# Two layers of graph convolution by dense count matrices: early gathers moved within the first tile, and the third sum's opening reordered

## The chip, the cores and the metric

The kernel runs on one core of one Trainium2 chip. The metric is device time in microseconds (us) of one execution. The core has five engines that run side by side: PE (TensorE, matrix products; PEld is its weight load), DVE (VectorE), ACT (ScalarE), POOL (GpSimd, which here issues the indirect gathers) and SP (SyncE, which here issues most other transfers). Each engine works through its own instructions in a fixed order, and an instruction whose data are not there holds up everything behind it on its engine.

## The reference

The graph has 6,250 nodes with 64 features and 206,250 directed edges (100,000 drawn ones, both ways, and one loop for each node), sorted by destination. Cut to what matters:

```python
h = relu(layernorm(x))
a = segment_sum(h[src], dst)                    # first sum
h = relu(relu((h + a) @ W1 + b1) @ W2 + b2)
a = segment_sum(h[src], dst)                    # second sum
x = x + relu((h + a) @ W3 + b3) @ W4 + b4
h = relu(layernorm(x))
y = relu(relu(h @ WM1 + bM1) @ WM2 + bM2) @ WM3 + bM3
z = segment_sum(y[src], dst)                    # third sum
out = x + relu(relu(concat(h, z) @ WU1 + bU1) @ WU2 + bU2) @ WU3 + bU3
```

The three sums run over the same edges. The message network of the second convolution depends on the source node alone, so it is computed per node.

## The kernel before

A sum over edges is a product with a matrix of counts, `A`, whose cell says how often an edge joins two nodes. The nodes make 49 tiles of 128. The kernel builds `A` tile by tile in bytes, uses each tile at once for the first sum, and stores it to DRAM (L429); the second and third sums read it back.

**Building.** A half tile of 64 destinations has its edges in a window of at most 120 neighbouring edges, and so 25 gather steps of 128 windows serve the 49 tiles. They come in thirteen batches (one step, then two each). For a batch `search` (L291) finds by ACT, among samples of `dst`, the block of 550 edges in which a window starts (L298), and DVE writes `row` and `base` (L302, L303). `fetch_blocks` (L306) lets POOL gather the blocks `blk` (L311). `search_block` (L315) counts in the block by ACT (L322). `fetch_edges` (L326) lets DVE compute the offset (`off_f` L331, `off` L332) and POOL gather the edges themselves (`d_win`, `s_win`, L336). `slots` (L342) takes them apart on DVE (from `pair`, L359), `cast` and `turn` bring them into `lkw`. For each tile `hot` makes one-hot patterns on DVE (`there` L400, `high` L404, `low` L407), PE counts by 64 products (`cnt`, L423), ACT evicts the counts (`a`, L425), and PE multiplies the 49 pieces of the tile with `hp`, the normalised features in three bfloat16 parts (`acc`, L566). `values` (L487) makes `hp` from `x` for seven tiles at a time: a norm, and `split` (L244 to L248), alternating between ACT and DVE.

**What sets the order.** Python code emits the instructions in a certain order; `beside` holds, for each quarter of each tile, the steps of later batches that are emitted beside it. A scheduler of the tile framework then fixes the order on each engine by data and by its own estimate of durations; `follow`, `behind` and `placed` tie some instructions to others. POOL's queue takes the gathers in the resulting order.

Batches in the start: the searches and gathers of batches 0 to 2 are emitted ahead of the first tile, with the values of five of the seven strips of `x`. Beside tile 0 come the last two strips, `search_block` and `fetch_edges` of batch 2, `search` and `fetch_blocks` of batch 3, and `search` of batch 4. Beside tile 1 (batch 1 in `beside`) come `search_block` and `fetch_edges` of batch 3 and `fetch_blocks` of batch 4.

**Second and third sum.** `sweep` goes over groups of four tiles (eleven of them, then one of three and one of two, L77). A group has 13 pieces of four steps each, the last with one step (the last group has six of eight steps and one of one). For a piece SP loads the counts as bytes (`a`, L731; five buffers), ACT or DVE widens them (`ar`, L735; six buffers), and PE multiplies (L742). A group sums in one PSUM bank, of two in `pacc`. After a group come its layers: `conv2` after the second sum, in six parts, and `conv3` after the third, in four; a part is emitted after so many further pieces as the tuple `after` says. `conv2` leaves `yr`, the stationary operand of the third sum; `conv3` frees its bank by ACT's copy (L697) and DVE's addition into `hz` (L698), and ends in an output transfer (L710). In the third sum the last two pieces of groups 0 and 1 wait until both groups' other eleven are done, because they need `yr` of the last five tiles. The layers of the last group of each sum are emitted after the sweep, all parts one after the other. The pool `f_pmix`, two banks that the first part uses, lies idle in the sweeps.

Of the kernel before, what the change touches and what calls it, by code (L numbers as in the profile page):

```python
# [151 lines left out]
def fast(ctx: ExitStack, tc: tile.TileContext, x, src, dst, w, bad, out):  # L152
# [138 lines left out]
    def search(b, after=None):  # L291

        if b >= len(BATCHES):
            return
        each, qs = tiles_of(b)
        for q in each:
            junk = wins.tile([P, NB], BF, name="junk", bufs=1)
            op = nc.scalar.activation(junk, smp, AF.Sign, bias=below_node[:, q:q + 1], accum_out=sign1[:, q:q + 1])  # L298
            if after:
                behind(op, after)  # L300
            follow(op, "ACT")
        nc.vector.tensor_scalar(row[:, qs], sign1[:, qs], -0.5, NB / 2 - 1, op0=OP.mult, op1=OP.add)  # L302
        return op, nc.vector.tensor_scalar(base[:, qs], sign1[:, qs], -0.5 * BLK, (NB / 2 - 1) * BLK + BLK / 2,  # L303
                                           op0=OP.mult, op1=OP.add)
# [10 lines left out]
    def search_block(b, i):  # L315

        if b >= len(BATCHES):
            return
        q = starts[b] + i
        blk = blks.pop(q)  # L320
        junk2 = wins.tile([P, BLK], BF, name="junk2", bufs=1)
        op = nc.scalar.activation(junk2, blk, AF.Sign, bias=below_node[:, q:q + 1], accum_out=sign2[:, q:q + 1])  # L322
        follow(op, "ACT")
        return op

    def fetch_edges(b):  # L326

        if b >= len(BATCHES):
            return
        each, qs = tiles_of(b)  # L330
        nc.vector.scalar_tensor_tensor(off_f[:, qs], sign2[:, qs], -0.5, base[:, qs], op0=OP.mult, op1=OP.add)  # L331
        nc.vector.tensor_scalar(off[:, qs], off_f[:, qs], float(E - P), None, op0=OP.min)  # L332
        lists[b] = [wins.tile([P, MOST, P], I32, name=name)[:, :len(each), :] for name in ("d_win", "s_win")]
        for win, of in zip(lists[b], (dst, src)):
            for i, q in enumerate(each):
                nc.gpsimd.indirect_dma_start(  # L336
                    out=win[:, i, :], out_offset=None, in_=of.rearrange("(a o) -> a o", o=1),
                    in_offset=bass.IndirectOffsetOnAxis(ap=off[:, q:q + 1], axis=0))
# [148 lines left out]
    def values(t):  # L487
        h = work.tile([P, XT, D], FP, name="h")
        begun, centered, squared = norm(h, t, XT)
        if t <= XT:  # L490
            behind(begun, sampled)
            behind(begun, bounds)
            behind(squared, searched[0])
        if t == XT:
            behind(centered, searched[1])
        split(hp[:, t:t + XT], h, XT, D)
# [3 lines left out]
    for b in range(len(BATCHES)):  # L500
        step = BATCHES[b]

        def at(u, what, *args):
            beside.setdefault(8 * starts[b] + u * step // 2, []).append((what, args))

        at(0, slots, b + 1)
        at(4, cast, b + 1, 0)
        at(5, cast, b + 1, 2)
        for i in range(BATCHES[b + 1] if b + 1 < len(BATCHES) else 0):
            at(7 + 2 * i, turn, b + 1, i)  # L510
        if b == 1:
            for i in range(BATCHES[3]):
                at(1 + i, search_block, 3, i)
            at(3, fetch_edges, 3)
            at(3, fetch_blocks, 4)
        if b > 0:
            at(6, search, b + 4)
            for i in range(BATCHES[b + 3] if b + 3 < len(BATCHES) else 0):
                at(10 + 2 * i, search_block, b + 3, i)
            at(13, fetch_edges, b + 3)  # L520
            at(14, fetch_blocks, b + 4)
# [24 lines left out]
    values(2 * XT)  # L546
    search(2, op)
    fetch_blocks(2)
    for t in range(3 * XT, 5 * XT, XT):
        values(t)  # L550

    r1, acc1 = {}, {}

# [32 lines left out]
    for t in range(NT + 1):  # L586
        last_total, total = total, FirstSum(t - 1, a) if t else None
        if t < NT:
            def between(i):
                if total:  # L590
                    total.quarter(i)
                if last_total and i == 2:
                    last_total.check()
                for what, args in beside.get(4 * t + i, ()):
                    what(*args)

            a = build(t, between)
            if t == 0:
                values(5 * XT)
                for i in range(2):  # L600
                    search_block(2, i)
                fetch_edges(2)
                values(6 * XT)
                search(3)
                fetch_blocks(3)
                search(4)
            if t == 1:
                w1p = weight_halves(w.w1x, "w1p", once)
                m1p = weight_halves(w.m1x, "m1p")
        else:  # L610
            last_total.check()
            for i in range(4):
                total.quarter(i)
            total.check()
# [8 lines left out]
    work = ctx.enter_context(tc.tile_pool(name="f_work2", bufs=2))  # L623
    narrow = ctx.enter_context(tc.tile_pool(name="f_narrow", bufs=5))
    wide = ctx.enter_context(tc.tile_pool(name="f_wide", bufs=6))
    pmix = ctx.enter_context(tc.tile_pool(name="f_pmix2", bufs=4, space=bass.MemoryType.PSUM))
    yr = late.tile([P, NT, 2, D], FR, name="yr")
    hz = late.tile([P, ROWS], FP, name="hz")

# [80 lines left out]
                queue.dma_start(out[ds(t0 * P, (k - 1) * P + m)].rearrange("(t p) d -> p t d", p=m),  # L710
                                o[:m, t0 - t:t0 - t + k, :])

    def sweep(stationary, self_too, late, single, then, after):

        accs = {}

        def width(g):

            return KC * (2 if GROUPS[g][1] <= 2 else 1)

        def piece(g, c):

            (t, n), k0 = GROUPS[g], c * width(g)
            if c == 0:
                accs[g] = pacc.tile([P, CH], FP, name="acc")
            acc = accs[g]
            m = min(width(g), H - k0)
            a = narrow.tile([P, 4 * KC * P], U8, name="a")[:, :n * m * P].rearrange("p (t b) -> p t b", t=n)  # L730
            nc.sync.dma_start(a, A[t:t + n, :, k0 * P:(k0 + m) * P].rearrange("t p b -> p t b"))  # L731
            ar = wide.tile([P, KC * 4 * P], FR, name="ar")[:, :m * n * P].rearrange("p (k t b) -> p k t b", t=n, b=P)
            widen = nc.scalar.copy if c % 5 in (1, 3) else nc.vector.tensor_copy
            order = "p k t b" if m % 2 == 0 else "p t k b"
            widen(ar.rearrange(f"p k t b -> {order}"), a.rearrange(f"p t (k b) -> {order}", b=P))  # L735
            for k in range(k0, k0 + m):
                if self_too and t <= k < t + n:
                    own = ar[:, k - k0, k - t, :]
                    nc.vector.tensor_tensor(own, own, w.ident, op=OP.add)
                parts = stationary(k)  # L740
                for i, part in enumerate(parts):
                    op = nc.tensor.matmul(acc[:, :n * P], part, ar[:, k - k0].rearrange("p t b -> p (t b)"),  # L742
                                          start=(k == 0 and i == 0), stop=(k == H - 1 and i == len(parts) - 1))
            swept[:] = [op]

        pieces, end = (H + KC - 1) // KC, len(GROUPS) - 1
        order = [(g, c) for g in range(end + 1) for c in range((H + width(g) - 1) // width(g))]
        if late:
            order[:2 * pieces] = sorted(order[:2 * pieces], key=lambda x: (x[1] >= pieces - 2, x))
        going = []  # L750
        for g, c in order:
            piece(g, c)
            for work_of in going:
                while work_of[1] and work_of[1][0] <= 0:
                    work_of[1].pop(0)
                    next(work_of[0], None)
                work_of[1] = [u - 1 for u in work_of[1]]
            if c == pieces - 1 and g < end - 1:
                going.append([then(*GROUPS[g], accs[g]), list(after)])
            elif g == end and c == 1:  # L760
                swept.clear()
                for _ in then(*GROUPS[end - 1], accs[end - 1]):
                    pass
        swept.clear()
        t, n = GROUPS[end]
        m = 1 if single else n
        works = [then(t + j, m, accs[end][:, j * P:(j + m) * P]) for j in range(0, n, m)]
        while works:
            works = [parts for parts in works if next(parts, works) is None]

    sweep(lambda k: [h2r[:, k, i, :] for i in range(2)], True, False, False, conv2, (0, 2, 5, 7, 9, 11))
    sweep(lambda k: [yr[:, k].rearrange("p i d -> p (i d)")], False, True, True, conv3, (0, 4, 8, 11))


@with_exitstack
# [248 lines left out]
```

## Time and profile before

| what | value |
|---|---|
| median of 3 runs | 888.64 us (888.33 to 889.93) |
| the profiled execution's own time | 890.53 us |
| its span, first to last instruction | 888.7 us |
| PE busy | 836.7 us (94%) |
| DVE busy | 636.3 us (72%) |
| ACT busy | 568.9 us (64%) |
| POOL busy | 119.2 us (13%) |
| products of second and third sum (L742) on the chain that ended last | 47% of the span |
| products of the first sum (L566) on it | 20% |

Busy time is an average over stages. The slices in the prediction cut the span into 40 parts of 22.2 us; a digit is the busy share in tenths, 9 meaning 90% or more. In a line of the timeline stand the start in us, the duration in us, engine, line, operation, what is written and read, how many instructions are merged, and in brackets the idle time before it with what ended it. "PEclk" and the granted clock are shares of TensorE's full clock. The first sum runs until about 382 us, the second until about 698, the third to about 880.

### The profile page before, as it was taken

The numbers are of one execution on the slowest core, as the hardware profiler recorded it, in microseconds if no ns is written. First come the engines' busy times: TensorE is split into PE (matmuls) and PEld (weight loads), VectorE is DVE, ScalarE is ACT, GpSimd is POOL, SyncE is SP. The second block draws the span as 40 slices with busy tenths as digits, with TensorE's granted clock in tenths as the row PEclk, the third lists the DMA queues.
The fourth block names the chain that finished last, engine by engine and source line by source line (L and its number), as shares of the span: only waits on it lengthen the run. The fifth ranks groups of instructions, "written<-read, shape, count | busy, mean of one in ns | idle before, by whom it ended". The sixth has DMA issues, their size and how long they took to land.

```text
span 888.7 us, 19590 instructions
## 1 busy us (share of the span) xinstructions
PE 836.7 (94%) x8202; PEld 727.9 (82%) x8202; DVE 636.3 (72%) x946; ACT 568.9 (64%) x768; POOL 119.2 (13%) x86
## 2 busy tenths in 40 slices
PE   0379999999999999999999999999999989999997
PEld 0369999999999999978888888888889867777786
DVE  6989999999999998635554545554556766677673
ACT  5557777767776666655555555555555677878873
POOL 3356544244322200000000000000000000000000
PEclk9989999999999999999999999999999999999998
DMA  6234343354443332745444444444435678898982
GB/s 146 74 137 160 148 172 135 135 184 149 158 147 139 123 146 111 220 107 134 122 122 127 124 123 122 130 111 127 130 96 135 168 195 208 237 244 235 248 219 67
DMA packets 192087, 133.57 MB, mean 150 GB/s; under 512 B 34965, under 2 KB 183317, under 8 KB 191989
## 3 DMA queue, kind: packets, MB, share of 16 engines
q1 hardware_dynamic: 185544, 121.19, 46.2%
q0 software_dynamic: 3600, 10.32, 4.1%
q8 instruction: 66, 1.08, 0.5%
q10 hardware_dynamic: 2844, 0.72, 0.4%
q14 instruction: 33, 0.26, 0.1%
HBM read 91.25 MB, written 40.94 MB: 149 GB/s over the span
## 4 chain that ended last, share of the span: by engine, by line
PE 88%; DVE 5%; DMA 3%; ACT 1%; issue 1%; POOL 1%; SPq 0%; ACTq 0%; POOLq 0%; DVEq 0%
PE acc L742 47%; PE acc L566 20%; PE cnt L423 8%; PE ps_t L445 6%; PE ps_y L454 4%; DVE low L407 1%; PE ps_g L484 1%; DMA blk<-in_dst_dram,row 1%; DVE high L404 1%; DVE there L400 1%; POOL s_win L336 1%; DMA d_win<-in_dst_dram,off 1%; ACT ar L735 1%; DMA xs<-in_x_dram 1%; PE tf L436 1%
## 5 line engine op out<-in xcount | busy, mean ns | idle before, releaser
L735 DVE CAST ar<-a 128x2048 fp32r<-128x2048 uint8 (+1 forms) x200 | 220.4, 1110 | 184.4 <-PE acc L742 157.0
L735 ACT CAST ar<-a 128x2048 fp32r<-128x2048 uint8 (+2 forms) x126 | 232.3, 1846 | 118.7 <-PE acc L742 100.0
L742 PE MATMUL acc<-ar,h2r 128*128 128x512 f32 (+2 forms) x1274 | 297.5, 388 | 0.0
L742 PEld LDWEIGHTS acc<-ar,h2r 128*128 128x128 f32 x1274 | 229.3, 188 | 49.7 <-issue 5.8
L566 PE MATMUL acc<-hp,a 128*128 128x193 bf16 x2401 | 239.1, 249 | 4.6 <-ACT a L425 2.3
L425 ACT ACTIVATE a<-cnt 128x784 int16<-128x784 f32 x196 | 161.0, 823 | 81.4 <-PE cnt L423 80.7
L566 PEld LDWEIGHTS <-a 128*128 128x128 fp8e4 x2401 | 198.9, 98 | 6.6 <-ACT a L425 2.9
L742 PE MATMUL acc<-ar,yr 128*128 128x512 f32 (+2 forms) x637 | 159.9, 402 | 2.5 <-DVE hz L698 1.3
L742 PEld LDWEIGHTS acc<-ar,yr 128*128 128x128 f32 x637 | 116.3, 190 | 35.2 <-issue 10.3
L423 PE MATMUL cnt<-high,low 128*128 128x49 bf16 x3136 | 113.8, 186 | 15.8 <-DVE low L407 13.2
L423 PEld LDWEIGHTS <-low 128*128 128x128 fp8e4 x3136 | 106.8, 96 | 23.5 <-DVE low L407 14.1
L407 DVE TENSOR_TENSOR low<-there,lkw 128x2048 int32<-128x2048 bf16 (+2 forms) x51 | 112.1, 2197 | 0.0
L404 DVE TENSOR_TENSOR high<-high,lkw 128x3136 bf16<-128x3136 bf16 (+2 forms) x51 | 87.7, 1720 | 15.0 <-PE cnt L423 14.5
L311 POOL DMA_INDIRECT blk<-in_dst_dram,row x25 | 53.4, 2137 | 90.6 <-DVE base L303 78.0
L400 DVE TENSOR_TENSOR there<-word,lkw 128x2048 bf16<-128x2048 bf16 (+2 forms) x51 | 59.0, 1173 | 0.0
L336 POOL DMA_INDIRECT d_win<-in_dst_dram,off x25 | 27.2, 1087 | 82.2 <-DVE pair L359 48.5
L336 POOL DMA_INDIRECT s_win<-in_src_dram,off x25 | 36.3, 1454 | 7.6 <-issue 7.6
L447 ACT ACTIVATE t<-ps_t,d 128x512 f32<-128x512 f32 (+2 forms) x26 | 17.3, 665 | 11.2 <-PE ps_t L445 11.1
L389 PE MATMUL ps_win<-identb,parts 128*128 128x128 bf16 x75 | 8.9, 225 | 15.7 <-ACT parts L381 15.7
L447 ACT ACTIVATE t<-ps_t,e 128x512 f32<-128x512 f32 (+2 forms) x28 | 17.6, 632 | 8.7 <-PE ps_t L445 8.7
L447 ACT ACTIVATE t<-ps_t,c 128x512 f32<-128x512 f32 (+1 forms) x26 | 17.1, 663 | 7.8 <-PE ps_t L445 7.8
L322 ACT ACTIVATE junk<-blk,below_node 128x550 bf16<-128x550 int32 x25 | 18.7, 747 | 2.6 <-DMA blk<-in_dst_dram,row 2.6
(122 smaller groups left out, 581.4 us busy)
## 6 DMA issues: line engine op xcount, KB each, us to landing
a<-A SPq DMA_DIRECT2D x276, 256.0 KB, 3.1
A<-a SPq DMA_DIRECT2D x49, 784.0 KB, 3.6
a<-A SPq DMA_DIRECT2D x24, 192.0 KB, 2.6
a<-A SPq DMA_DIRECT2D x22, 64.0 KB, 3.1
out_dram<-o SPq DMA_DIRECT2D x11, 128.0 KB, 2.8
xs<-in_x_dram ACTq DMA_DIRECT2D x3, 224.0 KB, 5.3
xs<-in_x_dram SPq DMA_DIRECT2D x3, 224.0 KB, 5.3
blk<-in_dst_dram,row POOLq DMA_INDIRECT x25, 4.9
```

The source lines that it names most:

```text
L311: nc.gpsimd.indirect_dma_start(out=blks[q], out_offset=None, in_=dst.rearrange("(r b) -> r b", b=BLK), in_offset=bass.IndirectOffsetOnAxis ...
L336: nc.gpsimd.indirect_dma_start(out=win[:, i, :], out_offset=None, in_=of.rearrange("(a o) -> a o", o=1), in_offset=bass.IndirectOffsetOnAx ...
L400: nc.vector.tensor_tensor(there, word2[:, None, :, :].to_broadcast(shape), of(0)[:, :, None, :].to_broadcast(shape), op=OP.is_equal)
L404: nc.vector.tensor_tensor(high, high2[:, None, :, :].to_broadcast(shape), of(1)[:, :, None, :].to_broadcast(shape), op=OP.is_equal)
L407: counted["DVE"] = nc.vector.tensor_tensor(low.rearrange("p (g i) w -> p g i w", i=2), there.rearrange("p g w i -> p g i w"), of(2)[:, :, ...
L423: counted["PE"] = nc.tensor.matmul(ps[:, b, j * H:(j + 1) * H], low[:, g, :], high[:, g // 2, :, g % 2], start=True, stop=True)
L425: counted["ACT"] = nc.scalar.activation(a[:, :, k:k + 2 * PG].rearrange("p h (b j) -> p h b j", b=2), ps[:, :, :PG * H].rearrange("p b (j ...
L445: placed(nc.tensor.matmul(ps[:, :n * P], wt, rhs, start=(i == 0), stop=(i == len(terms) - 1)))
L447: nc.scalar.activation(to, ps[:, :n * P], AF.Relu, bias=bias)
L566: nc.tensor.matmul(acc[:, t % 2, :], self.a[:, k, :], hp[:, k], start=(k == 0), stop=False)
L735: widen(ar.rearrange(f"p k t b -> {order}"), a.rearrange(f"p t (k b) -> {order}", b=P))
L742: op = nc.tensor.matmul(acc[:, :n * P], part, ar[:, k - k0].rearrange("p t b -> p (t b)"), start=(k == 0 and i == 0), stop=(k == H - 1 and ...
```

## The change

Two things are changed. In the start, `search` and `fetch_blocks` of batch 3, and `search_block` and `fetch_edges` of batch 2, move ahead of the first tile; beside tile 0 now come `search_block` and `fetch_edges` of batch 3 and `fetch_blocks` of batch 4; the special case beside tile 1 goes.

In the third sum `late` becomes a number of groups, three instead of two, whose last two pieces come after all their others; the third of them sums in a bank of `f_pmix` (now called `more`). `sweep` takes a list `going` of layers that are still to be done: the second sum's last group hands its `conv2` to the third sweep, which emits its parts after 0, 2, 10, 14, 17 and 20 further pieces. In the third sum each group's `conv3` has its later parts put off by five pieces for each set of layers still going when it begins. The last group's layers are still emitted after the sweep, tile by tile.

```diff
-        if b == 1:
-            for i in range(BATCHES[3]):
-                at(1 + i, search_block, 3, i)
-            at(3, fetch_edges, 3)
-            at(3, fetch_blocks, 4)
...
     fetch_blocks(2)
-    for t in range(3 * XT, 5 * XT, XT):
-        values(t)
+    values(3 * XT)
+    search(3)
+    fetch_blocks(3)
+    values(4 * XT)
+    for i in range(2):
+        search_block(2, i)
+    fetch_edges(2)
...
             if t == 0:
                 values(5 * XT)
                 for i in range(2):
-                    search_block(2, i)
-                fetch_edges(2)
+                    search_block(3, i)
+                fetch_edges(3)
                 values(6 * XT)
-                search(3)
-                fetch_blocks(3)
                 search(4)
+                fetch_blocks(4)
...
-    pmix = ctx.enter_context(tc.tile_pool(name="f_pmix2", bufs=4, space=bass.MemoryType.PSUM))
+    more, pmix = pmix, ctx.enter_context(tc.tile_pool(name="f_pmix2", bufs=4, space=bass.MemoryType.PSUM))
...
-    def sweep(stationary, self_too, late, single, then, after):
+    def sweep(stationary, self_too, late, then, after, going):
...
-                accs[g] = pacc.tile([P, CH], FP, name="acc")
+                accs[g] = more.tile([P, CH], FP, tag="mix", name="acc") if 2 <= g < late else pacc.tile([P, CH], FP, name="acc")
...
-        if late:
-            order[:2 * pieces] = sorted(order[:2 * pieces], key=lambda x: (x[1] >= pieces - 2, x))
-        going = []
+        order[:late * pieces] = sorted(order[:late * pieces], key=lambda x: (x[1] >= pieces - 2, x))
         for g, c in order:
             piece(g, c)
-            for work_of in going:
+            for parts in going:
...
+            going = [parts for parts in going if parts[1]]
             if c == pieces - 1 and g < end - 1:
-                going.append([then(*GROUPS[g], accs[g]), list(after)])
+                spread = 5 * len(going) if late else 0
+                going.append([then(*GROUPS[g], accs[g]), [u + spread * (u > 0) for u in after]])
...
-        t, n = GROUPS[end]
-        m = 1 if single else n
-        works = [then(t + j, m, accs[end][:, j * P:(j + m) * P]) for j in range(0, n, m)]
-        while works:
-            works = [parts for parts in works if next(parts, works) is None]
-
-    sweep(lambda k: [h2r[:, k, i, :] for i in range(2)], True, False, False, conv2, (0, 2, 5, 7, 9, 11))
-    sweep(lambda k: [yr[:, k].rearrange("p i d -> p (i d)")], False, True, True, conv3, (0, 4, 8, 11))
+        return accs[end]
+
+    t, n = GROUPS[-1]
+    acc = sweep(lambda k: [h2r[:, k, i, :] for i in range(2)], True, 0, conv2, (0, 2, 5, 7, 9, 11), [])
+    going = [[conv2(t, n, acc), [0, 2, 10, 14, 17, 20]]]
+    acc = sweep(lambda k: [yr[:, k].rearrange("p i d -> p (i d)")], False, 3, conv3, (0, 4, 8, 11), going)
+    going = [conv3(t + j, 1, acc[:, j * P:(j + 1) * P]) for j in range(n)]
+    while going:
+        going = [parts for parts in going if next(parts, going) is None]
```

More of the change, by code (lines that the diff above doesn't have):

```diff
@@ L747, in sweep @@
         order = [(g, c) for g in range(end + 1) for c in range((H + width(g) - 1) // width(g))]
-        if late:
-            order[:2 * pieces] = sorted(order[:2 * pieces], key=lambda x: (x[1] >= pieces - 2, x))
-        going = []
+        order[:late * pieces] = sorted(order[:late * pieces], key=lambda x: (x[1] >= pieces - 2, x))
         for g, c in order:
             piece(g, c)
-            for work_of in going:
[L754 to L757, printed above, removed]
+            for parts in going:
+                while parts[1] and parts[1][0] <= 0:
+                    parts[1].pop(0)
+                    next(parts[0], None)
+                parts[1] = [u - 1 for u in parts[1]]
+            going = [parts for parts in going if parts[1]]
             if c == pieces - 1 and g < end - 1:
-                going.append([then(*GROUPS[g], accs[g]), list(after)])
+                spread = 5 * len(going) if late else 0
+                going.append([then(*GROUPS[g], accs[g]), [u + spread * (u > 0) for u in after]])
             elif g == end and c == 1:
```

## The prediction, made before the changed kernel was run

> **What bounds the kernel now.** I read the slices first, to see which engine is full where, then the timeline at the two places that the diff touches, then busy time by stage.
>
> ```profile
> PE   0379999999999999999999999999999989999997
> DVE  6989999999999998635554545554556766677673
> PEclk9989999999999999999999999999999999999998
> ```
>
> A slice is 22.2 us. PE is full from the fifth slice to the end, apart from one slice at about 710 us; the first four belong to DVE. The list of PE's waits is empty between 90 and 690 us. So time can change in the start (0 to 90 us), at the passage from the second sum to the third (698 to 748 us) and in the tail. What the start loses, PE does not make up.
>
> The start, from the timeline:
>
> ```profile
> 28.29 1.30 POOL L336 DMA_INDIRECT s_win<-in_src_dram,off  x1 [0.30 <-issue]
> 29.22 0.69 DVE L407 TENSOR_TENSOR low<-there,lkw 128x512 int32<-128x512 bf16 x1
> 29.82 0.29 DVE L359 TENSOR_SCALAR pair<-d_win 128x256 int32<-128x256 int32 x1
> 29.89 1.04 POOL L311 DMA_INDIRECT blk<-in_dst_dram,row  x1 [0.30 <-issue]
> 31.23 0.95 POOL L311 DMA_INDIRECT blk<-in_dst_dram,row  x1 [0.30 <-issue]
> ...
> 51.96 2.42 PE L566 MATMUL acc<-hp,a 128*128 128x193 bf16 x14 [2.11 <-DVE hp L248]
> 55.83 0.29 DVE L366 TENSOR_SCALAR high_i<-s_win 128x256 int32<-128x256 int32 x1 [0.58 <-DMA s_win<-in_src_dram,off]
> 60.35 0.75 ACT L322 ACTIVATE junk<-blk,below_node 128x550 bf16<-128x550 int32 x1 [1.04 <-DMA blk<-in_dst_dram,row]
> 62.68 0.16 DVE L331 SCALAR_TENSOR_TENSOR off_f<-sign,base 128x2 f32<-128x2 f32 x1 [2.04 <-ACT junk L322]
> 89.60 0.59 PE L423 MATMUL cnt<-high,low 128*128 128x49 bf16 x16 [0.86 <-DVE low L407]
> ```
>
> POOL issues gathers back to back until 29.59, and batch two's blocks leave at 29.89 and 31.23. DVE is busy without a break until two short stops, 0.58 and 2.04 us, both on gathers. At 89.60 PE waits for DVE for the last time.
>
> How long a block takes from issue to landing (last number, for the one issued at 29.89):
>
> ```profile
> blk<-in_dst_dram,row POOLq DMA_INDIRECT x1, 3.4
> ```
>
> The passage, from the timeline, then by stretch (length, busy time of PE, PEld, DVE, ACT, POOL, then granted clock, DMA share, GB/s):
>
> ```profile
> 727.28 1.20 PE L742 MATMUL acc<-ar,yr 128*128 128x512 f32 x4 [1.12 <-DVE yr L253]
> 729.83 4.36 PE L742 MATMUL acc<-ar,yr 128*128 128x512 f32 x12 [1.35 <-DVE hz L698]
> ```
> ```profile
> 727.00:729.80 2.80, 1.20 (x4) 0.67 (x4) 2.18 (x4) 1.73 (x3) 0.00 (x0) 0.91 0.40 108
> 729.80:734.00 4.20, 4.17 (x12) 3.36 (x13) 3.64 (x4) 3.14 (x2) 0.00 (x0) 0.65 0.65 181
> 747.50:761.50 14.00, 14.00 (x64) 10.89 (x63) 9.43 (x10) 10.56 (x9) 0.00 (x0) 1.00 0.93 239
> ```
>
> PE stops twice, for `yr` of the last tiles and for the accumulator that `hz` frees, and then runs at a granted clock of 0.65. The last line is the steady third sum: one group in 14.0 us, PE full.
>
> **Part 1, the start: +6.1 us.** The edit takes out none of the work; it changes the order of instructions that the built programs show on each engine. In POOL's order batch three's two block gathers come ahead of batch two's edge gathers, and batch three's edge gathers ahead of batch four's blocks. On ACT the two searches in batch two's blocks (L322) move ahead of tile 0's first eviction; on DVE `off_f` of batch two moves ahead of `pair` of batch one, and the last `hp` part (L248) from before tile 2's `low` to after it.
>
> What they wait for has not moved: the gathers queued ahead of batch two's blocks are the same, so these still leave at 29.89 and 31.23 and land at 33.3 and, at the same 3.4 us, 34.6.
>
> DVE's lag. Both orders agree through `r` (L246) at 23.41, over at about 23.97. Then come twelve instructions up to tile 0's first `low`: by the starts of like rows 0.08+0.53+0.08+0.07+0.53+0.53+0.10+0.34+0.53+0.53+0.47+0.60 = 4.4, so 28.4. The next `r` needs ACT's cast of `h`, queued behind the first search. ACT: 33.3 + 0.85 (search and accumulator read, as at 14.39) + 0.55 (cast) = 34.7. DVE does `r` and the reciprocal (0.53+0.10), then `off_f` waits for the second search: 34.7 + 0.30 (`var`) + 0.85 = 35.85. Idle: 6.3 + 0.5 = 6.8. `pair` starts at 35.95, not 29.82, with two instructions of 0.53 still undone and 0.2 done that came later before: DVE is 6.13 + 1.06 − 0.2 = 7.0 behind. Then the two old stops go: batch two's edge gathers start at about 37.6 instead of 46.46, and batch three's blocks have long landed. 7.0 − 0.58 − 2.04 = 4.4 from then on.
>
> PE's lag. Fourteen products at 51.96 waited for the last two `hp` parts. With the lag the second of these comes at 62.85: tile 0's last `low` ends at 44.6; to tile 2's `there` 8.8 more, and to the end of its `low` 7.4, including 0.45 of waiting for ACT's casts, makes 60.85; then `r`, three batch instructions and the `hp` part, 2.0. Before, from PE's second seven of the fourteen (53.07: half-way by 2.22/14 us each) to 88.74, where it waits for tile 7's `low`, lie 35.67 us. Off: 1.63 and 0.20 of stops on ACT, and 1.0 for 33 counting products which the new order puts ahead. 62.85 + 32.85 = 95.7, where 89.60 stood: +6.1. Tile 7's `low`, at 89.56 + 4.4 = 94.0, or 95.1 with DVE's reductions waiting for the late PE, no longer decides. The slow clock of 52 to 57 us I keep. Bounds: DVE's own lag, +4.4, and the lag with nothing won back, +7.0. I take the walk, +6.1.
>
> The Trainium skill (DMA: Bandwidth & Descriptors, Anatomy of one DMA — SWDGE) gives 2.0 us plus bytes over 436 GB/s for a gather issued by GpSimd. For a block of 281.6 KB that is an estimate of 2.6 us where the trace has 3.4; by it the start would lose 0.8 us less.
>
> **Part 2, the passage: −3.2 us.** Group 2 of the third sum gets an accumulator of the idle `f_pmix` pool, so that 33 pieces instead of 22 run ahead of the last two of each group, and `conv2` of the last two tiles is spread over them. Both stops lose their cause: `yr` is wanted 44 products later (44 × 0.224 = 9.9 us), and group 3's accumulator is wanted 10 products, 2.2 us, after group 0 ends, for a copy of 0.58 and an addition of 0.69. From 726.16 (end of the products at 724.29) to 747.54 PE did 52 products, four layer products and two output products. At the steady rate (49, two and one in 14.0, with 10.98 for the 49) that is 11.65 + 6.04 = 17.7 us, not 21.4: at most 3.7 to win, about 1.7 of it clock (12 × 0.224 = 2.7 against 4.36).
>
> What can come in its place is late data: 33 pieces of 256 KB in 33 × 0.896 + 4.9 (layers of `conv2`) = 34.5 us are 250 GB/s, against 239 at a share of 0.93. I leave 0.5 for that and ask −3.2, between −3.7 and 0.
>
> The Trainium skill (TensorE: Matmul & The Clock Gate, Part 1) lets the clock fall after about 3.4 us of idleness. Here two stops of 1.12 and 1.35 us were followed by a clock of 0.65. By the rule the 1.7 would not belong to the stops, and part 2 would bring 2.0 at most.
>
> **Part 3, the layers in parts: −0.3 us.** `conv3` of most groups starts five pieces later per group still going, and the groups' layers interleave. Work and buffers stay; PE is full in the steady stretch, which also covers the later output transfers. In the tail PE has three waits, of 0.68, 0.17 and 0.16; group 10's last layers now fill some, while its output (128 KB) leaves later. Bounds −0.7 and +0.5. SP's order changes by when outputs come between loads only. `going` without finished entries and the moved return issue nothing.
>
> Sum: 6.1 − 3.2 − 0.3 = +2.6. The profiled execution took 890.53 (span 888.7), so 893.1 of its kind; it stands 1.9 above the median of the three runs, 888.64, and on that I put 891.2.
>
> **Rivals.** A measurement of this kernel can tell about 0.2%, 1.8 us.
> - *Only DVE's lag counts.* PE's order lets it catch up to DVE at tile 7: +4.4 − 3.5 = +0.9, 889.5, no change. For it: tile 7's `low` is at most 1.7 us earlier than PE. Against it: PE has no wait to give back.
> - *Faster: the blocks are there in time.* If batch two's first block is searched before DVE gets to `r` at 28.4, the start only wins, 0.58 + 2.04, and 888.64 − 2.6 − 3.5 = 882.5. The sign turns at a start loss of 3.5, 2.6 us less than I find. For it: `row` of batch two is ready at 22.6. Against it: POOL's four gathers until 29.59.
> - *The third sum gives nothing.* DMA, or `hz` behind a cast on ACT, takes the stops' place: 888.64 + 6.1 = 894.7. For it: casts wait for DMA in the steady stretch. Against it: in 698 to 748 us they wait mostly for PE.
>
> **How the numbers follow.** Forecast 50%, only DVE 22%, nothing in the third sum 15%, blocks in time 13%. Slower 65%, same 22%, faster 13%. The forecast's own range is 889.2 to 893.0: its 6.1 from 5.0 to 7.0, its 3.5 from 4.4 to 2.6. Eight in ten: leaving out the fast case and some of the ends, 887.2 to 895.2.
>
> **What would show it.** Step 1 is right if DVE's `r` or `off_f` waits about 6 us for ACT between 28 and 36 us, ACT waits there for `blk`, the stops of 0.58 and 2.04 are gone, and PE is without waits only from about 96 us. Part 2 is right if no wait on `yr` or `hz` stands at the passage and the clock stays at 1.00. I am wrong if the blocks leave POOL sooner, if PE's start depends less on the last `hp` part, or if casts wait for DMA in the 33 pieces.

## The result, and the profile after

The changed kernel takes 894.88 us (median of 6 runs, 891.8 to 896.51) against 889.44 for the kernel before beside it (median of 6): a ratio of 1.0054, 95% interval 1.0038 to 1.0071. It is 0.5% slower, some 4.8 us. The profiled execution took 895.18 us with a span of 893.4, 4.7 more than the 888.7 of before. The forecast was 891.2 with a range up to 895.2: the sign held, and the time lies in the range, 0.3 us under its upper end. Of the sum's three terms one held, one was twice too large, and one that was put at next to nothing cost 4.5 us.

The slices of the page of after:

```profile
PE   0179999999999999999999999999999999999996
DVE  6799999999999998635554545554455777666662
PEclk9989999999999999999999999999999999999999
```

The slice of PE at about 710 us that was not full is full now. The slow clock at the passage was too short to show in a slice of before; the clock's digit for the last slice is 9 where it was 8. DVE loses busy tenths in the second slice, the start.

The start, from the timelines of POOL, ACT, DVE and PE of after:

```profile
28.06 1.00 POOL L311 DMA_INDIRECT blk<-in_dst_dram,row  x1 [0.30 <-issue]
31.41 0.75 ACT L322 ACTIVATE junk<-blk,below_node 128x550 bf16<-128x550 int32 x1 [5.64 <-DMA blk<-in_dst_dram,row]
32.75 0.63 DVE L246 TENSOR_TENSOR r<-h,hp 128x448 f32<-128x448 f32 x1 [4.51 <-ACT hp L244]
33.82 0.17 DVE L331 SCALAR_TENSOR_TENSOR off_f<-sign,base 128x2 f32<-128x2 f32 x1 [0.33 <-ACT junk L322]
61.07 1.29 PE L566 MATMUL acc<-hp,a 128*128 128x193 bf16 x7
92.47 0.58 PE L423 MATMUL cnt<-high,low 128*128 128x49 bf16 x16
```

ACT waits 5.64 us for batch two's first block, and DVE waits behind it, 4.51 + 0.33 us. The old stops of 0.58 and 2.04 us are gone. PE starts the products that need the last `hp` part at 61.07 and has no wait for DVE after that; tile 7's counting, at 89.60 before, stands at 92.47, and DVE had its `low` ready at 91.25. The third sum's first product comes at 701.67 instead of 698.97: the start costs 2.7 to 2.9 us, not 6.1.

The passage, from PE's timeline of after:

```profile
728.16 13.26 PE L743 MATMUL acc<-ar,yr 128*128 128x512 f32 x56
741.60 1.19 PE L743 MATMUL acc<-ar,yr 128*128 128x512 f32 x4 [0.19 <-DVE hz L697]
```

The stop for `yr` is gone, that for `hz` is down from 1.35 to 0.19 us, and the granted clock stays at 1.00. All this is as forecast. And yet from the third sum's first product to the end of the span after needs 893.4 − 701.67 = 191.7 us, where before needed 888.7 − 698.97 = 189.7. Instead of winning 3.5 us the third sum lost 2.0. Where, PE's waits between 780 and 860 us say, a stretch in which PE of before has none (engine and line, what it waited for, us in total, times, longest):

```profile
PE ps_y L454 <- ACT t L447: 3.1, 5, 1.1
```

One of these, in the timelines of ACT and PE of after, in order of time:

```profile
832.77 1.89 ACT L736 CAST ar<-a 128x2048 fp32r<-128x2048 uint8 x1
833.14 1.02 PE L445 MATMUL ps_t<-t,u 128*128 128x512 f32 x2
834.68 0.58 ACT L696 COPY f<-acc 64x512 f32<-64x512 f32 x1
835.50 1.90 ACT L736 CAST ar<-a 128x2048 fp32r<-128x2048 uint8 x1 [0.24 <-DMA a<-A]
837.31 0.68 ACT L447 ACTIVATE t<-ps_t,e 128x512 f32<-128x512 f32 x1
838.04 1.10 PE L454 MATMUL ps_y<-u,t 128*128 128x64 f32 x8 [1.09 <-ACT t L447]
```

The same layer in before:

```profile
827.03 1.02 PE L445 MATMUL ps_t<-t,u 128*128 128x512 f32 x2
829.33 0.68 ACT L447 ACTIVATE t<-ps_t,e 128x512 f32<-128x512 f32 x1
830.68 1.00 PE L454 MATMUL ps_y<-u,t 128*128 128x64 f32 x8
```

In before the eviction of the second layer starts 2.30 us after its product, behind one cast, and has 0.67 us to spare. In after it starts 4.17 us after its product: the rest of a cast, the copy with which ACT empties the next group's bank, and a whole further cast stand ahead of it. PE has twelve products of cover (3.36 us) and then stands still. A stop costs more than its length: from one `ps_y` to the next lie 14.60, 14.91, 15.36 and 14.56 us, against 14.0 in before, 0.56 to 1.36 more, where the waits themselves are 0.32 to 1.09 us. The rows show the difference of about 0.26 us: in before `ps_y` starts 0.16 us ahead of the end of the products before it (827.49 + 3.35 against 830.68), which is lost at a stop, and it takes 1.10 us behind a stop instead of 1.00.

Why the layers lie there: `conv3` of a group is put off by five pieces for each set of layers still going. Its parts then come 9, 13 and 16 pieces after the group's end instead of 4, 8 and 11. A group has 13 pieces, so the layers are still going when the next group ends, that one is put off too, and so on to the last. The putting off begins in the opening and goes on through the sum.

### The profile page after: what moved, and what is told of

Its sections match the earlier page's. It is cut to its first block, busy times and chain, and to the rows that moved or that the text cites. A ratio compares the mean times of both kernels' runs of the same rounds, so it can differ in the third digit from the quotient of the medians.

```text
span 893.4 us, 19596 instructions
## 1 busy us (share of the span) xinstructions
PE 836.1 (94%) x8202; PEld 726.5 (81%) x8202; DVE 636.0 (71%) x946; ACT 567.1 (63%) x768; POOL 123.3 (14%) x86
## 3 DMA queue, kind: packets, MB, share of 16 engines
HBM read 91.25 MB, written 40.94 MB: 148 GB/s over the span
## 4 chain that ended last, share of the span: by engine, by line
PE 78%; DMA 9%; ACT 6%; DVE 4%; issue 2%; POOL 0%; SPq 0%; ACTq 0%; DVEq 0%; POOLq 0%
PE acc L743 36%; PE acc L566 23%; PE cnt L423 9%; DMA a<-A 7%; PE ps_t L445 4%; ACT ar L736 4%; PE ps_y L454 3%; DVE ar L736 2%; PE ps_g L484 1%; DMA blk<-in_dst_dram,row 1%; ACT t L447 1%; PE tf L436 1%; DMA xs<-in_x_dram 1%; ACT a L425 1%; PE acc L568 0%
## 5 line engine op out<-in xcount | busy, mean ns | idle before, releaser
L743 PE MATMUL acc<-ar,yr 128*128 128x512 f32 (+2 forms) x637 | 157.8, 399 | 0.2 <-DVE hz L697 0.2
L311 POOL DMA_INDIRECT blk<-in_dst_dram,row x25 | 58.4, 2337 | 99.8 <-DVE base L303 87.7
L389 PEld LDWEIGHTS <-parts 128*128 128x128 bf16 x75 | 5.8, 98 | 17.5 <-ACT parts L381 17.5
```

Source lines behind the costliest of these rows:

```text
L311: nc.gpsimd.indirect_dma_start(out=blks[q], out_offset=None, in_=dst.rearrange("(r b) -> r b", b=BLK), in_offset=bass.IndirectOffsetOnAxis ...
```

## The experiments

**Theory 1**: the passage wins what was forecast, and the putting off of layers, which keeps itself alive, loses it again, because of the order on ACT at the group's end. **Theory 2**: the 33 pieces ahead, with their loads, are to blame, or the passage's gain was never there. For the start: the cost is the wait for batch two's blocks, or the changed order of `hp` and `low` around tile 2 (the last `hp` part now comes after tile 2's `low`). Ratios are to the kernel before, on the same chip, with 95% intervals; 0.1% is 0.9 us. A difference of two such ratios has an interval of some 0.16 to 0.2% either way, 1.4 to 1.8 us.

### The start alone, and the third sum alone

`start_only` is before with the first part of the change's diff, `third_only` before with the second.

> The kernel before with the edit of the start alone. My prediction's walk: +6.1 us, PE's last wait for DVE at the start at about 95.7 us instead of 89.60. By the trace of after, where PE reached tile 7's counting 2.9 us late and the third sum began 2.7 us late: +2.8 us (+0.3%), last wait of PE before about 62 us. If only the two removed stops of DVE counted: -2.6 us. Whether POOL issues batch two's blocks at about 28.1 (as in after) or 29.9 us (as in before) shows whether that difference belongs to the edit or to the run.

Measured: 1.0061 (1.0043 to 1.0080), 5.4 us over. The third sum begins at 701.58, as in after, so 2.6 of the 5.4 lie in the start. The rest lies behind it: this third sum is before's own, but takes 894.4 − 701.58 = 192.8 us. PE's timeline at the passage of `start_only`:

```profile
730.51 1.20 PE L741 MATMUL acc<-ar,yr 128*128 128x512 f32 x4 [1.12 <-DVE yr L253]
733.06 5.49 PE L741 MATMUL acc<-ar,yr 128*128 128x512 f32 x12 [1.34 <-DVE hz L697]
```

The stops are those of before to a hundredth, but the twelve products behind them take 5.49 us instead of 4.36: here the clock stayed low for twice as long. It is so in more than the profiled execution: the six executions of `start_only` have a mean granted clock of 0.989 to 0.991, the nineteen of before beside them 0.991 to 0.996. (More on that in the last section.) POOL issues batch two's blocks at 28.00, as in after.

> The kernel before with all edits of the third sum and the old start. Prediction: -3.5 us (-3.2 at the passage, -0.3 in the tail). By the trace of after (third sum 191.7 us from its first product to the end of the span, before 189.7): +2.0 us, made of about -3.5 at the passage, +4.5 in groups 4 to 8, where the last layer's products wait for ACT once per group, and +0.7 to +1.0 in the last groups.

Measured: 1.0008 (0.9997 to 1.0020). The third sum takes 888.6 − 698.87 = 189.7 us, as in before: the 2 us of loss that after shows are not there in full, but neither is any of the gain. The groups' waits are there, somewhat shorter:

```profile
818.65 1.10 PE L454 MATMUL ps_y<-u,t 128*128 128x64 f32 x8 [0.79 <-ACT t L447]
833.48 1.11 PE L454 MATMUL ps_y<-u,t 128*128 128x64 f32 x8 [0.58 <-ACT t L447]
```

### Layers put off only in the opening

```diff
-                spread = 5 * len(going) if late else 0
+                spread = 5 * len(going) if g < late else 0
```

> As third_only, but layers are put off only for groups 0 to 2; from group 3 on they stand 4, 8 and 11 pieces after the group's end, as before. Theory 1 (putting off keeps itself alive: layers at 9, 13 and 16 pieces outlast the next group's 13 pieces, so the second layer's eviction on ACT stands behind the next group's copy and a cast that waits for its load, and PE waits in order): the waits of PE for ACT in groups 4 to 8 go, a group takes 14.0 us again, and the time is 2.8 to 3.5 us under before. Theory 2 (the 33 pieces run ahead leave the loads late for the rest of the sum, or the passage's gain was never there): the waits stay or others come, and the time is 0 to +2 us.

Measured: 0.9970 (0.9955 to 0.9985), 2.7 us under before. The waits between 780 and 860 us are gone, and groups take 13.99 us:

```profile
826.70 1.00 PE L454 MATMUL ps_y<-u,t 128*128 128x64 f32 x8
840.69 1.00 PE L454 MATMUL ps_y<-u,t 128*128 128x64 f32 x8
```

The third sum takes 884.8 − 697.92 = 186.9 us, 2.8 less than before. Theory 1 holds: the passage's gain is real, with all 33 pieces ahead, and what ate it are the layers of the later groups. The opposite edit shows the same from the other side: before, with nothing but the putting off.

```diff
-                going.append([then(*GROUPS[g], accs[g]), list(after)])
+                spread = 5 * sum(1 for job in going if job[1]) if late else 0
+                going.append([then(*GROUPS[g], accs[g]), [u + spread * (u > 0) for u in after]])
```

> The kernel before with one edit: its third sum puts layers off by five pieces for each group still going. 22 pieces run ahead as before, and the last two tiles' layers stay together. Theory 1: groups take 14.6 to 15.4 us instead of 14.0 from about group 3 on, with one wait of PE for ACT in each, and the time is 4 to 6 us over before, the stops of 1.12 and 1.35 us at the passage unchanged. Theory 2 (the 33 pieces or the loads are the cause): within 1 us of before.

Measured: 1.0080 (1.0057 to 1.0103), 7.1 us over, more than I allowed. The stops at the passage are unchanged; PE waits in seven groups, from group 2 on, and mostly longer than in after, such as here, where the group took 15.35 us:

```profile
840.12 1.11 PE L454 MATMUL ps_y<-u,t 128*128 128x64 f32 x8 [1.01 <-ACT t L447]
```

### Which instruction on ACT it is

Two edits of `third_only` that leave the putting off in all groups, and take the whole cast from ahead of the eviction. In the first the second layer comes one piece earlier; ACT's order is then copy, eviction, cast, where it was copy, cast, eviction.

```diff
-    acc = sweep(..., False, 3, conv3, (0, 4, 8, 11), going)
+    acc = sweep(..., False, 3, conv3, (0, 4, 7, 11), going)
```

> As third_only (all edits of the third sum, layers still put off in all groups), but the second layer comes 12 pieces after the group's end instead of 13, so that on ACT its eviction stands right behind the next group's copy and no longer behind a cast after it. Theory 1 (PE waits because that one cast, and the load it waits for, are ahead of the eviction): the waits of PE for ACT in groups 4 to 8 go, a group takes 14.0 us, and the time is 2.5 to 3.5 us under the kernel before, as third_first3. Rival (layers that reach into the next but one group are late whatever stands on ACT): 0.2 to 1.1 us of wait per group stay, as in third_only, and the time is within 1.5 us of before.

Measured: 1.0014 (0.9999 to 1.0030). I expected 2.5 to 3.5 us under, and missed. PE's waits at `ps_y` are gone in all groups, as theory 1 says, but the second layer's own product, which comes a piece earlier, waits for the first layer's eviction in some of them, for up to 1.39 us:

```profile
828.37 1.13 PE L445 MATMUL ps_t<-t,u 128*128 128x512 f32 x2 [1.39 <-ACT t L447]
```

That eviction stands behind a cast which itself waits 2.88 us for PE to free a buffer. So the edit moved the wait rather than removed it, and told less than I wanted. The second edit moves no layer: it gives the one cast in question, piece 6's, to DVE.

```diff
-            widen = nc.scalar.copy if c % 5 in (1, 3) else nc.vector.tensor_copy
+            widen = nc.scalar.copy if c % 5 in (1, 3) and not (late and c == 6) else nc.vector.tensor_copy
```

> As third_only (layers put off in all groups, second layer 13 pieces after), but in the third sum the widening of piece 6, the cast that stands on ACT between the next group's copy and the second layer's eviction, is done by DVE (1.2 us more per group there, 1.9 less on ACT). Theory 1: the waits of the last layer's products for ACT go, a group takes 14.0 us, and the time is 2 to 3.5 us under before, as third_first3. Rival (layers so late are always caught by something, as in second_at_12): other waits take their place, and the time is within 1.5 us of before.

Measured: 0.9972 (0.9962 to 0.9983). No wait of PE is left between 780 and 860 us, and groups take 13.97 us. From the timelines of ACT and PE:

```profile
843.18 0.69 ACT L447 ACTIVATE t<-ps_t,e 128x512 f32<-128x512 f32 x1 [0.43 <-PE ps_t L445]
845.76 1.00 PE L454 MATMUL ps_y<-u,t 128*128 128x64 f32 x8
```

Now ACT waits for PE ahead of the eviction, and not the other way round. One cast of 1.9 us on ACT in each group, at that place, is what the putting off cost. Late layers as such are no harm. ACT has less to do in this run, too, but a full ACT was not the trouble: in after it is busy for 11.21 us of the longest group's 15.36. A run that moves the cast to another place on ACT was not made.

### Which part of the opening wins

`third_first3` with two groups ahead instead of three; the last tiles' `conv2` is still handed over and spread.

```diff
-    acc = sweep(..., False, 3, conv3, (0, 4, 8, 11), going)
+    acc = sweep(..., False, 2, conv3, (0, 4, 8, 11), going)
```

> As third_first3, but only 22 pieces run ahead (no accumulator from the idle pool), with the layers of the last two tiles still spread over them. If each stop of the passage has the cause I gave it: the stop for yr (1.12 us) goes, the one for the accumulator that hz frees (1.35 us) stays, and the time lies between third_first3 and before, 1 to 2 us under before; a slow clock after the stop may cost up to 3 us of it. If the layers' spreading does all of it: as third_first3, 2.5 to 3 us under before.

Measured: 1.0000 (0.9989 to 1.0011). Both stops stand, against my expectation that the one for `yr` would go:

```profile
726.23 1.20 PE L744 MATMUL acc<-ar,yr 128*128 128x512 f32 x4 [1.12 <-DVE yr L253]
728.77 4.55 PE L744 MATMUL acc<-ar,yr 128*128 128x512 f32 x12 [1.34 <-DVE hz L698]
```

The whole gain, 0.30%, comes with the third accumulator and the eleven pieces that it lets run ahead. The handing over alone wins nothing; the third accumulator without it was not run.

### What the start pays for

`after_first3` is the changed kernel with the repair of `third_first3`: against that kernel it has the start's edit, and no stops at the passage that could bring the clock in.

> The changed kernel with one repair: layers are put off only for groups 0 to 2. It is third_first3 with the start's edit, so the start's cost is seen without the stops at the passage and the slow clock that may follow them. If the start costs what the traces of after and start_only show at the third sum's first product (2.7 us): 889.5 to 890.5 us, no difference from before. If it costs the 5.4 us by which start_only was longer in time: 892 to 893 us, 0.3 to 0.4% over before.

Measured: 1.0003 (0.9992 to 1.0014), against 0.9970 without the start's edit: the start costs 0.33%, 2.9 us (some 1.7 either way), what the traces show. Against the changed kernel, 1.0054, the one line of repair is worth 0.5%, 4.5 us. In the profile its third sum takes 887.5 − 701.29 = 186.2 us, where that of after takes 191.7.

`blocks_first` is `start_only` with batch two's blocks gathered before batch one's edges:

```diff
     for i in range(2):
         op = search_block(1, i)
-    fetch_edges(1)
-    turn(0, 0)
-    values(2 * XT)
     search(2, op)
     fetch_blocks(2)
+    fetch_edges(1)
+    turn(0, 0)
+    values(2 * XT)
```

> start_only with the block gathers of batch two ahead of the edge gathers of batch one on POOL, so that they leave at about 23 us instead of 28. If the start's cost is the wait for these blocks (DVE 4.8 us for ACT, ACT for the gather): the wait shrinks to under 1 us, DVE's waits for batch one's edges stay under 2 us, the third sum's first product comes at 697 to 699 us, and the time is within 2 us of before. If the cost is the changed order of hp and low around tile 2: PE's early waits and the 2.7 us stay, and the time is 3 to 6 us over, as start_only.

Measured: 1.0015 (1.0000 to 1.0030), 1.3 us over before and 4.1 under `start_only`. The block leaves POOL at 22.27, ACT does not wait for it, and DVE's one wait in that stretch is for batch one's edges (timelines of ACT and DVE):

```profile
25.68 0.75 ACT L322 ACTIVATE junk<-blk,below_node 128x550 bf16<-128x550 int32 x1
31.99 0.29 DVE L366 TENSOR_SCALAR high_i<-s_win 128x256 int32<-128x256 int32 x1 [1.57 <-DMA s_win<-in_src_dram,off]
```

The third sum begins at 699.19, where it begins between 697.91 and 699.72 in the seven profiles with the old start. With the repaired third sum:

> after_first3 with the same order of gathers as blocks_first. If the wait for the blocks is the start's cost, as third_first3: 886 to 888 us, 0.2 to 0.4% under before. If it is the order of hp and low: as after_first3.

Measured: 0.9975 (0.9964 to 0.9987), against 1.0003 with the blocks late. By time, both pairs say that most of the start's cost is the wait for the blocks. This one puts it at about 2.5 us; the other's 4.1 also holds the shorter slow clock at the passage. By the third sum's first product the profiles have it smaller here (700.35 against 701.29) than there (699.19 against 701.58).

`start_gathers` leaves the searches in batch two's blocks where they were, and moves only batch three's search and block gathers up:

```diff
-    for t in range(3 * XT, 5 * XT, XT):
-        values(t)
+    values(3 * XT)
+    search(3)
+    fetch_blocks(3)
+    values(4 * XT)
...
                 values(6 * XT)
-                search(3)
-                fetch_blocks(3)
                 search(4)
```

> The kernel before with half of the start's edit: the search and the block gathers of batch three move up to the first values; the searches in batch two's blocks and its edge gathers stay beside tile 0's end, so that ACT does not wait for blocks while DVE has work. If the wait on ACT is what the start pays: no stop of DVE for ACT near 28 us, the old stop of 2.04 us for batch three's blocks gone, and 1 to 2.5 us under before. If the search's own instructions ahead of tile 0 cost as much as the stop: within 1 us of before. If what the edit cost lies in the order of the gathers: 2 to 5 us over.

Measured: 1.0023 (1.0011 to 1.0035), 2.0 us over; I expected a gain. DVE has no wait for ACT near 28 us, but it has others later: the stop for batch three's blocks is still 1.25 us, and PE waits early for what the new order puts late:

```profile
54.40 1.51 PE L423 MATMUL cnt<-high,low 128*128 128x49 bf16 x32 [2.42 <-DVE low L407]
```

> start_gathers and third_first3 in one kernel. If the two gains add: 4 to 5 us under before (884.5 to 885.5 us). If the start gives nothing: as third_first3, 2.5 us under.

Measured: 0.9987 (0.9975 to 0.9999), again about 0.2% over the kernel that differs by the same edit, `third_first3`, though this second difference lies within its noise. So by the times moving the search up costs 1.5 to 2 us even without the wait for batch two's blocks. By the third sum's first product, 699.36 and 698.94, the two profiles do not show it. The order of `hp` and `low` around tile 2, which `start_gathers`, `blocks_first` and after share, would explain it, but no run here holds that order alone. What goes with the order is a slow clock: between 50 and 64 us it is at 0.50 for 10.24 us in both profiles with this start, for 6.82 to 6.84 in the five with the start of after or of `blocks_first`, and for 3.40 to 3.42 in six of the seven with the old start (6.82 in before). The nine executions of `start_gathers` have a mean granted clock of 0.989 to 0.993, the thirty of before beside them 0.990 to 0.997. So PE's early waits and the slow clock behind them are the likely cause, and not a shown one. `blocks_first3`, with the same order, is only 0.05% over `third_first3`, a difference within the noise.

The best kernels of the study are `third_first3` (0.9970) and `cast6_dve` (0.9972), with before's start, the third accumulator and no cast ahead of the late eviction, and `blocks_first3` (0.9975). All three beat before and after; they can't be told from each other.

## Why the prediction was right, and where it was wrong

Put together from the time ratios, the change is the start with +2.9 us (`after_first3` against `third_first3`), the opening of the third sum with −2.7 (`third_first3` against before) and the putting off with +4.5 (after against `after_first3`). These are steps from before to after through two kernels, so that their sum, the measured +4.8 but for rounding, proves nothing by itself. The forecast had +6.1, −3.2 and −0.3, which is +2.6. Its errors of −3.2, +0.5 and +4.8 us partly cancel, and to that extent it is luck that the time lies in the range: with the start at 6.1 the same kernel would have taken some 898 us, an estimate from these steps, and the range ended at 895.2.

**The start: right mechanism, half the size.** The waits came where I put them: ACT for `blk`, DVE for ACT between 28 and 34 us, the two old stops gone. Mis-sized were two terms of the walk.
- DVE's idle time: 6.8 forecast, 4.51 + 0.33 = 4.84 measured. I took the blocks' issue at 29.89 from before's trace, "the gathers queued ahead of batch two's blocks are the same, so these still leave at 29.89". They are the same, but took 1.50 and 0.94 us instead of 2.84 and 1.30, and the block left at 28.06. From issue to search lay 3.35 us: the trace's 3.4 held, and not the 2.6 that I estimated from the Trainium skill (DMA: Bandwidth & Descriptors, Anatomy of one DMA — SWDGE).
- PE's way from the last `hp` part to tile 7: 32.85 forecast, 92.47 − 61.07 = 31.40 measured. Together with the part's coming 1.78 earlier (61.07 for 62.85) this is 3.2, the whole gap between 6.1 and 2.9. About half of the 1.45 is the clock, which I kept: of the way from the part on, 3.8 us are at half speed in before and 2.3 in after, by an estimate 0.75 us of products. The profile of before is no measure of it, since its slow stretch is 6.82 us long and that of the six others with its start 3.40 to 3.42.

Two numbers of one profiled execution thus went into the sum as if the kernel had set them. The lower bound I gave, 4.4, fell for the same reason: it was worked out from the same 29.89. DVE's `low` for tile 7 ended 1.7 us later than before (91.25 for 89.55).

**The passage: right.** Forecast −3.2 between −3.7 and 0; −2.7 by the time, −2.8 and −3.5 by the profiles of `third_first3` and `after_first3`. The part that I ascribed to the clock is the doubtful one: it depends on the execution. `start_gathers` has the old passage with both stops and no slow clock, and its third sum takes 888.1 − 699.36 = 188.7 us; against 186.2 to 186.9 that leaves 1.8 to 2.5 us for the stops themselves.

**The layers in parts: the step that failed.** "Work and buffers stay; PE is full in the steady stretch" put them between −0.7 and +0.5. They cost 4.5 in the changed kernel (3.4 with the old start, `third_only` against `third_first3`; 7.1 in the kernel before, `spread_only`). The prediction followed work and buffers. It did not write out ACT's order at the group's end, where the new place of the second layer puts a bank copy and a whole cast ahead of the eviction that PE waits for. PE's own order looks harmless (24, 13, 12 products of the sum between the layers' products instead of 21, 16, 12), and that the putting off lasts was no surprise ("`conv3` of most groups starts five pieces later"); what it does to ACT's order was not asked. One reading of the tail was off and carries nothing: PE's waits there are 0.68, 0.19 and 0.24 us, and the 0.17 and 0.16 are those of its weight loads.

**The rivals.** The third sum as a whole gave nothing, and the time, 894.88, is that rival's 894.7; but its mechanism, loads or `hz` in place of the stops, is not what happened, and its start of 6.1 was wrong. "Only DVE's lag counts" did not occur: PE has no wait for DVE from 61.07 up to tile 7, whose `low` is ready 1.2 us early. Nor did "the blocks are there in time"; `blocks_first` shows what that would have needed, batch two's gathers ahead of batch one's, and even there the start won nothing (third sum from 699.19, for 698.97 in before).

## What to carry to other kernels

When a step of one engine moves, write out the order on every engine that serves it, and count what stands ahead of the piece that is waited for: here 3.36 us of matmuls no longer covered a copy and two casts. A rule that puts work off "while other work is going" must be followed for several rounds, since it can feed itself. And a time read from one execution, such as a gather's, is a sample: the like rows of that trace (0.94 to 2.84 us for such a gather) should have set the bounds.

## What was not expected of the hardware

The clock after the passage's stops. Six profiled executions have both stops, 1.12 and 1.34 or 1.35 us long, and differ in what follows. Three of their stretches (length, busy time of PE, PEld, DVE, ACT, POOL, then granted clock, DMA share, GB/s), of before:

```profile
729.00:733.00 4.00, 3.17 (x8) 2.55 (x9) 3.71 (x5) 3.07 (x3) 0.00 (x0) 0.57 0.41 108
```

of `start_only`:

```profile
733.00:740.00 7.00, 6.94 (x16) 4.99 (x17) 4.20 (x5) 3.35 (x3) 0.00 (x0) 0.56 0.74 195
```

and of `spread_only`:

```profile
729.00:733.00 4.00, 2.65 (x12) 1.95 (x11) 3.94 (x5) 3.96 (x4) 0.00 (x0) 1.00 0.46 125
```

Summed over stretches of one microsecond, the clock is at 0.50 for 3.42, 3.40 and 3.42 us in before, `handed_two` and `blocks_first`, for 6.84 in `start_only`, and not at all in `spread_only` and `start_gathers`. In the eight profiles without the two stops it does not fall there. The Trainium skill (TensorE: Matmul & The Clock Gate, Part 1) says that the clock is either half or full and is set by a free-running window of about 3.4 us. The lengths of the drops, one such window, two or none, agree, as do those in the start (3.40 to 3.42, 6.82 to 6.84 and 10.24 us); that a fall wants a whole idle window does not, since here two stops with 1.20 us of products between them were enough, in four executions of six. What a short stop costs can therefore not be read from one profile: the same stop was followed by nothing, or by 3.4 or 6.8 us at half speed.

The first of POOL's gathers of batch one's sources took 2.83 or 2.84 us in four profiles with the old start, 0.94 in three others with the same start, and 1.50 or 1.51 in the five that move batch three's search up and leave batch two's blocks behind batch one's edges. What decides this stays open.

The Trainium skill (Perfetto Trace Analysis, Optimization Strategy) says that the same gap coming back through a stretch, on the engine that should be full, can mean too few buffers. Here the gap came back in every group, and no buffer was short: with the same buffers, one cast given to another engine took it away (`cast6_dve`).
